# The last chunk of a graph layer with experts: slot tiles and sorting earlier, placing later, and a copy moved from VectorE to ScalarE

## The chip, the cores and the metric

The kernel runs on one core of a Trainium2 chip. The time is the device time of one execution in microseconds (us); the time of the kernel before is the median of three runs. The engines are called by their names in the profile: PE (TensorE), DVE (VectorE), ACT (ScalarE), POOL (GpSimd), and SP, whose queue issues plain DMAs. Each engine works through its own instructions in the order of the program.

## What is computed

The input has 6250 nodes of 256 features (x) and 100000 edges (src, dst), sorted by dst. All arithmetic is float32.

```python
h = layernorm(x)
agg = segment_sum(h[src], dst) / maximum(deg, 1)          # mean over a node's incoming edges
x = x + concat([h, agg], axis=1) @ W.T + b                # the graph layer
xn = layernorm(x) * gamma + beta                          # the feed-forward layer
top2 of (xn @ Wr + br) among 8 experts, softmax over the two
y_e = gelu(xn @ W1[e] + b1[e]) @ W2[e] + b2[e]            # 256 -> 512 -> 256
x = x + sum of the two chosen y_e, weighted
```

## The kernel before

**Windows, chunks, batches.** The edges are cut into 784 tiles of 128. Fourteen tiles make a window (a run of at most 128 consecutive destination nodes), 56 windows in all; four windows make a chunk, 14 chunks. For every edge tile POOL gathers 128 rows of the transformed nodes from DRAM (`gather`, L624) into one of 28 buffers `xg`, and PE adds them to the window's sums with a one-hot matrix (`add_edges`, L641). A gather reuses the buffer of the gather 28 places before it.

**From a finished chunk to its experts.** `window_done` plans the steps of a chunk. They are counted from its last edge tile: normalising, routing to two experts (`route`, `choices`), counting how many tokens each expert gets (`count_tokens`). Then, for each of the four windows, `one_hot_slots` (L719 to L722, DVE, two instructions into a tile `to`) builds the one-hot matrix that sorts the window's tokens by expert, and `sort_tokens` (L728 on PE, L731 on ACT) applies it and writes the sorted tokens to `xs`. On DVE `share_runs`, `place_rest` and `place_runs` work out where each expert's run of tokens goes. `copy_runs` (L872, ACT, eight groups of four copies, each group behind a load of registers) copies the runs to their places in `xe`. `find_rows` (L822, L826 to L835) works out for each token the rows of the results that it will need, `put_plan` (L839, SP, four times) writes that plan to DRAM, each at a row that depends on the data, and `load_plans` (L854) reads it back by node.

**Experts.** Each expert has a share of 128 slots in a chunk: `hidden` (L897 on PE, Gelu at L902 on ACT) and `result` (L910 on PE, bias at L914 on DVE, then a write to `y_d` through SP). Tokens beyond a share are collected over a batch of chunks into extra tiles. The batches are of 8, 5 and 1 chunks, with 8, 5 and 2 extra tiles. `more_stages` works on these tiles in three parts: `one` (L940: first product on PE; L944: a copy of it from PSUM to SBUF), `two` (L949: four transposes on PE; L952: Gelu on ACT) and `three` (L958: second product on PE; L962: bias on DVE; L965: write to `y_d` through SP). The PSUM tiles `ph` and `pm` have two buffers each, `py` has one. The five extra tiles of the second batch are called T0 to T4 here.

**Adding up.** When a batch is complete, its nodes can be finished in tiles of 128 nodes, n0 to n48: 27 tiles after the first batch, 18 after the second, 4 after the third. `gather_rows` reads the node's row (L986, SP) and issues two gathers of result rows on POOL (L989); `add_rows` makes two weighted additions on DVE (L996) and writes the output (L998, SP). The three buffers of a node tile come in turn from the same 28 `xg`, so the first gather of node tile n reuses the buffer from which the output of tile n-9 was written.

**The order of the work** is written by hand. For each edge tile, and after the last of them for further steps, `after` does this: first what was planned for the step with `at`, then expert tasks from a list as far as a budget of estimated us allows, then additions and gathers of finished nodes. The last chunk has its own step numbers in `LastSteps`: `hot` and `sort` for the four windows, `runs`, `rest` and `place` for the three placing functions, `copied` for the first `copy_runs` (one more group per step, `pace`), `rows` for `find_rows`, the plan writes one per step (`apart`) from `rows + 1`, `start` for the chunk's experts. What stands in the same step goes in the order in which it was planned: the slot tiles and sorts first, then placing, copying, rows, plan writes, and after all that the expert tasks. During the last chunk's steps the rest of chunk 12's experts and T0 to T4 are on the task list.

Of the kernel before, what the change touches and what calls it, by code (L numbers as in the profile page):

```python
# [8 lines left out]
F32 = mybir.dt.float32  # L9
I32 = mybir.dt.int32  # L10
AF = mybir.ActivationFunctionType
# [6 lines left out]
P = 128  # L18
# [4 lines left out]
CW = 4  # L23
# [10 lines left out]
def gnn_ffn_kernel(ctx: ExitStack, tc: tile.TileContext, x, x_cols, src, dst, dst_next, gw, gw_t, gb, gb_cols, gamma, beta,  # L34
# [35 lines left out]
    nc = tc.nc  # L70
# [542 lines left out]
    work = fast_pools.enter_context(tc.tile_pool(name="work", bufs=2, side="right"))  # L613
# [102 lines left out]
        nc.vector.tensor_scalar(q2, q2, -1.0, None, op0=ALU.add)  # L716

    def one_hot_slots(G, i):
        to = work.tile([P, 2 * P], F32, name="to", bufs=3)  # L719
        nc.vector.tensor_scalar(to, cols, G.to[:, 0, i:i + 1], None, op0=ALU.is_equal)  # L720
        nc.vector.scalar_tensor_tensor(to, cols, G.to[:, 1, i:i + 1], to, op0=ALU.is_equal, op1=ALU.add)  # L721
        G.one_hot[i] = to  # L722
# [155 lines left out]
    def in_turn(items, of):  # L878

        return [(us, f, of) for t in range(len(items) + 2) for d in range(3)  # L880
                if 0 <= t - d < len(items) and d < len(items[t - d]) for us, f in items[t - d][d]]
# [47 lines left out]
    def more_stages(B):  # L929

        def one(T):
            if T.first == 0:
                _, B.regs = nc.values_load_multi_w_load_instructions(
                    B.expert[0:1, :], engines=(ET.PE, ET.DVE, ET.Activation), min_val=0, max_val=NX - 1,
                    skip_runtime_bounds_check_because="clamped to it")
            T.e = B.regs[T.first]
            at = B.at + T.first * XS
            ph = ps.tile([P, H], F32, name="ph")
            for k in range(KD):
                nc.tensor.matmul(ph, xe[:, k, at:at + P],  # L940
                                 w1_sb[:, bass.ds(T.e, 1), k, :].rearrange("p a h -> p (a h)"),
                                 start=(k == 0), stop=(k == KD - 1))
            T.pre = slots.tile([P, H], F32, name="rows", bufs=3)
            nc.vector.tensor_copy(T.pre, ph)  # L944

        def two(T):
            pt = ps.tile([P, KH, P], F32, name="ph")
            for c in range(KH):
                nc.tensor.transpose(pt[:, c, :], T.pre[:, c * P:(c + 1) * P], ident)  # L949
            T.hid = slots.tile([P, KH, 2 * P], F32, name="hid")  # L950
            for c in range(KH):
                nc.scalar.activation(T.hid[:, c, :P], pt[:, c, :], AF.Gelu,  # L952
                                     bias=b1_sb[:, bass.ds(T.e, 1), c:c + 1].rearrange("p a c -> p (a c)"))

        def three(T):
            py = ps.tile([P, 2, D], F32, name="py", bufs=1)
            for c in range(KH):
                nc.tensor.matmul(py[:, 0, :], T.hid[:, c, :P],  # L958
                                 w2_sb[:, bass.ds(T.e, 1), c, :].rearrange("p a d -> p (a d)"),
                                 start=(c == 0), stop=(c == KH - 1))  # L960
            ys = slots.tile([P, 2, D], F32, name="rows", bufs=3)
            nc.vector.tensor_tensor(ys[:, 0, :], py[:, 0, :],  # L962
                                    b2_sb[:, bass.ds(T.e, 1), :].rearrange("p a d -> p (a d)"), op=ALU.add)
            at = B.more_row + T.first * XS
            nc.sync.dma_start(y_d[at:at + P, :], ys[:, 0, :])  # L965
            B.left -= 1

        items = []
        for i in range(B.tiles):
            T = Group()  # L970
            T.first = i
            items.append([[(1.7, lambda T=T: one(T))], [(0.5, lambda T=T: two(T))], [(1.75, lambda T=T: three(T))]])
        return in_turn(items, B)
# [32 lines left out]
    class Steps:  # L1006

        x1, var, roots, norms, route, exps, weigh, choices, count = 2, 5, 7, 9, 11, 14, 15, 16, 19
        hot, sort = (22, 24, 26, 28), (26, 28, 30, 32)
        runs, rest, place, tiles, copied, rows, pace, start, apart = 30, 33, 36, 39, 40, 46, 1.5, 60, 2  # L1010

    class LateSteps:

        x1, var, roots, norms, route, exps, weigh, choices, count = 2, 4, 5, 7, 9, 11, 12, 13, 15
        hot, sort = (17, 18, 20, 22), (19, 21, 23, 25)
        runs, rest, place, tiles, copied, rows, pace, start, apart = 20, 22, 24, 27, 26, 28, 1.25, 36, 1

    class LastSteps:

        x1, var, roots, norms, route, exps, weigh, choices, count = 2, 4, 5, 6, 7, 8, 9, 10, 12  # L1020
        hot, sort = (13, 14, 17, 18), (15, 16, 19, 20)
        runs, rest, place, tiles, copied, rows, pace, start, apart = 15, 16, 19, 24, 21, 22, 1, 29, 1

    def at(t, f, *args):
        later.setdefault(max(t, now), []).append(lambda: f(*args))
# [1 line left out]
    def window_done(V, G, K, t):  # L1027
# [26 lines left out]
        for m in range(CW):  # L1054
            at(t + S.hot[m], one_hot_slots, G, m)
            at(t + S.sort[m], sort_tokens, G, m)
# [134 lines left out]
    with tc.If(wrong_r > 0), tc.tile_pool(name="gp", bufs=1) as gp:  # L1191
# [9 lines left out]
        with tc.For_i(0, W * C) as j:  # L1201
# [22 lines left out]
            to = gp.tile([P, 1], I32, name="to")  # L1224
# [107 lines left out]
```

## Time and profile before

| | us |
|---|---|
| Three runs | 1191.4, 1193.38, 1197.1 |
| Median | 1193.38 |
| The profiled execution's own time | 1191.66 |
| Its span (first to last instruction) | 1189.9 |
| PE / DVE / ACT / POOL busy | 1056.3 / 691.0 / 465.4 / 844.3 |
| Mean granted clock of PE (1 is full) | 0.956 |

A line of the order in time holds the start in us from the span's start, the duration in us, the engine, the line of the kernel, the operation, what it writes and reads, the count, and in brackets the idle time of the engine before it with what ended it. An engine with a "q" is its queue's own work, such as issuing a DMA; the duration of such a line is that of issuing, not of the transfer. A line of the waits names who waited for whom, the sum in us, how often, and the longest. A line of the groups has busy time, mean ns of one instruction, and idle time before.

### The profile page before, as it was taken

The page shows a single profiled execution, that of the slowest core. Times are in us where ns is not written, and L with a number is a line of the kernel's source. Part 1 is how long each engine was busy: PE and PEld are TensorE (multiplying, and loading weights), DVE is VectorE, ACT ScalarE, POOL GpSimd, SP SyncE. Part 2 cuts the span into 40 slices and gives each one's busy share as a digit, 9 for nine tenths or more (in the row PEclk, how much of TensorE's full clock was granted, in tenths as well). Part 3 has the DMA queues.
Part 4 walks back from the last instruction along what each step waited for, and adds up shares of the span by engine and source line. Part 5 has one row for each costly group of instructions (what it writes and reads, how often), then busy time and mean ns, then how long its engine had stood idle before and what let it go on. Part 6 is the DMA issues. An engine that isn't in the chain of part 4 may idle for free.

```text
span 1189.9 us, 18885 instructions
## 1 busy us (share of the span) xinstructions
PE 1056.3 (89%) x5352; PEld 853.5 (72%) x5352; DVE 691.0 (58%) x2428; ACT 465.4 (39%) x1282; POOL 844.3 (71%) x892
## 2 busy tenths in 40 slices
PE   7959996599989899898998979899999999997970
PEld 6747873488868678685877858578888888785750
DVE  5858897365736555463565537465572745657642
ACT  3330013435444434443453444434553543643510
POOL 0077777777777777777777777777777777777575
PEclk9989997899999999998999999999999999998995
DMA  9988978856564554546456465555656565677784
GB/s 322 350 274 265 289 220 267 259 142 144 143 146 140 139 141 137 136 138 147 131 147 135 140 133 144 136 144 140 141 135 158 144 137 143 144 209 218 206 249 131
DMA packets 143578, 210.08 MB, mean 177 GB/s; under 512 B 36652, under 2 KB 111128, under 8 KB 143340
## 3 DMA queue, kind: packets, MB, share of 16 engines
q0 software_dynamic: 42768, 118.91, 40.6%
q1 hardware_dynamic: 92364, 80.45, 21.1%
q10 hardware_dynamic: 8336, 9.45, 2.4%
q8 instruction: 45, 0.74, 0.3%
q14 instruction: 65, 0.53, 0.2%
HBM read 163.86 MB, written 44.86 MB: 175 GB/s over the span
## 4 chain that ended last, share of the span: by engine, by line
PE 67%; DMA 15%; DVE 8%; issue 4%; ACT 3%; POOL 2%; ACTq 1%; POOLq 0%; SPq 0%; DVEq 0%
PE pS L641 23%; PE ph L897 15%; PE py L910 14%; DMA xg<-z_d,src_i 6%; DMA xg<-y_d,plans 4%; PE pm L728 4%; ACT xe L872 2%; PE ph L271 2%; PE pm L271 2%; PE pS L644 2%; PE py L958 2%; DMA plan_d<-plan 1%; PE ph L940 1%; DVE xg L996 1%; DMA xg<-x_dram,src_i 1%
## 5 line engine op out<-in xcount | busy, mean ns | idle before, releaser
L624 POOL DMA_INDIRECT xg<-z_d,src_i x770 | 732.8, 952 | 234.8 <-issue 111.0
L641 PE MATMUL pS<-xg,hot 128*128 128x265 f32 x1540 | 432.1, 404 | 42.0 <-DMA xg<-z_d,src_i 37.8
L641 PEld LDWEIGHTS pS<-xg,hot 128*128 128x128 f32 x1540 | 280.1, 194 | 127.3 <-DMA xg<-z_d,src_i 63.9
L897 PEld LDWEIGHTS ph<-xe,w_sb 128*128 128x128 f32 x1792 | 221.1, 196 | 23.9 <-ACT hid L902 10.2
L897 PE MATMUL ph<-xe,w_sb 128*128 128x128 f32 x1792 | 223.9, 280 | 13.7 <-ACT hid L902 9.8
L910 PE MATMUL py<-w_sb,hid 128*128 128x256 f32 x896 | 214.5, 383 | 1.7 <-DVE rows L914 1.7
L635 DVE TENSOR_TENSOR hot<-cols,rel 128x896 f32<-128x896 f32 x110 | 119.7, 1088 | 142.8 <-PE pS L641 140.2
L902 ACT ACTIVATE hid<-ph,b_sb 128x128 f32<-128x128 f32 x448 | 127.9, 369 | 172.3 <-PE ph L897 172.0
L910 PEld LDWEIGHTS py<-w_sb,hid 128*128 128x128 f32 x896 | 169.1, 191 | 33.3 <-issue 6.7
L872 ACT ACTIVATE xe<-xs x448 | 140.0, 313 | 98.3 <-ACT xe L872 32.6
L989 POOL DMA_INDIRECT xg<-y_d,plans x98 | 95.9, 978 | 37.9 <-issue 15.9
L731 ACT ACTIVATE xs<-pm,beta_sb,gamma_sb 128x256 f32<-128x256 f32 x112 | 57.3, 562 | 134.6 <-PE pm L728 132.1
L914 DVE TENSOR_TENSOR rows<-py,b_sb 128x512 f32<-128x512 f32 x56 | 38.4, 687 | 111.8 <-PE py L910 111.8
L728 PE MATMUL pm<-to,xn 128*128 128x256 f32 x224 | 58.8, 385 | 5.4 <-DVE to L721 5.4
L663 ACT ACTIVATE sums<-pS 128x265 f32<-128x265 f32 x55 | 21.4, 389 | 106.7 <-PE pS L641 99.2
L683 DVE SCALAR_TENSOR_TENSOR x<-pS,rdeg,x 128x264 f32<-128x264 f32 x55 | 27.1, 493 | 56.2 <-DMA x<-u_d 54.8
L996 DVE SCALAR_TENSOR_TENSOR xg<-xg,plans,xg 128x256 f32<-128x256 f32 (+1 forms) x98 | 45.8, 483 | 21.2 <-DMA xg<-y_d,plans 19.4
L271 PE MATMUL ph<-gc,x_t 128*128 128x264 f32 (+1 forms) x200 | 56.6, 407 | 1.4 <-ACT zt L295 0.9
L902 ACT ACT_TABLE_LOAD x25 | 32.1, 1283 | 64.7 <-PE ph L897 55.1
L339 POOL DMA_INDIRECT xg<-x_dram,src_i x14 | 13.5, 961 | 61.6 <-DMA src_i<-src_dram 57.6
L271 PE MATMUL pm<-gc,x_t 128*128 128x264 f32 (+1 forms) x192 | 53.1, 400 | 1.4 <-DVE u_t L425 1.4
L728 PEld LDWEIGHTS pm<-to,xn 128*128 128x128 f32 x224 | 42.7, 192 | 14.1 <-issue 4.7
(214 smaller groups left out, 908.0 us busy)
## 6 DMA issues: line engine op xcount, KB each, us to landing
y_d<-rows SPq DMA_DIRECT2D x56, 256.0 KB
xg<-z_d,src_i POOLq DMA_INDIRECT x770, 3.1
w_sb<-w_dram ACTq DMA_DIRECT2D x16, 512.0 KB
x<-u_d SPq DMA_DIRECT2D x55, 132.0 KB
x_d<-x SPq DMA_DIRECT2D x55, 128.0 KB
u_d<-u_t SPq DMA_DIRECT2D x24, 264.0 KB
x_t<-x_cols_dram SPq DMA_DIRECT2D x12, 512.0 KB
xu<-x_dram SPq DMA_DIRECT2D x24, 256.0 KB
```

The lines of the kernel that those rows point to most:

```text
L271: nc.tensor.matmul(pz, x_t[:, t, k, :], gc[:, h * KD + k, :n], start=(k == 0), stop=(k == KD - 1))
L624: nc.gpsimd.indirect_dma_start(out=xg[(g * C + c) % XG][:, :DZ], out_offset=None, in_=z_d[:, :], in_offset=bass.IndirectOffsetOnAxis(ap=sr ...
L635: nc.vector.tensor_tensor(hot, col[:, None, :].to_broadcast([P, HC, P]), V.rel[:, c:c + HC, None].to_broadcast([P, HC, P]), op=ALU.is_equal)
L641: nc.tensor.matmul(V.pS, V.hot[c // HC][:, c % HC, :], xg[(V.g * C + c) % XG], start=(c == 0), stop=(c == C - 1))
L728: nc.tensor.matmul(px[:, k, :], G.xn[i][:, k * P:(k + 1) * P], G.one_hot[i], start=True, stop=True)
L731: nc.scalar.activation(xs[:, at:at + 2 * P], px[:, k, :], AF.Identity, bias=beta_sb[:, k:k + 1], scale=gamma_sb[:, k:k + 1])
L872: nc.scalar.activation(xe[:, :, bass.ds(to_at, CAP)], src[:, :, bass.ds(src_at, CAP)], AF.Copy)
L897: nc.tensor.matmul(ph[:, i, a * SH:(a + 1) * SH], w1_sb[:, U.e + a, k, c * P:(c + 1) * P], xe[:, k, at:at + SH], start=(k == 0), stop=(k = ...
L902: nc.scalar.activation(U.hid[:, c, a * SH:(a + 1) * SH], ph[:, i, a * SH:(a + 1) * SH], AF.Gelu, bias=b1_sb[:, U.e + a, c:c + 1])
L910: nc.tensor.matmul(U.py[:, h, :], U.hid[:, c, h * P:(h + 1) * P], w2_sb[:, U.e + h, c, :], start=(c == 0), stop=(c == KH - 1))
L989: nc.gpsimd.indirect_dma_start(out=V.y2[r], out_offset=None, in_=y_d[:K.batch.end_row, :], in_offset=bass.IndirectOffsetOnAxis(ap=plans[:c ...
L996: nc.vector.scalar_tensor_tensor(V.o, V.y2[r], plans.bitcast(F32)[:count, n, 2 + r:3 + r], V.o, op0=ALU.mult, op1=ALU.add)
```

## The change

Three things are altered. The slot tile `to` has four buffers (`CW` is 4) where it had three. The copy of an extra tile's first product goes to ScalarE; it is the same line for all fifteen extra tiles. And the last chunk's step numbers are other ones: the four slot tiles stand in steps 13, 13, 14 and 15, the sorts in 14 to 17, the placing functions in 16, 17 and 18 where they were in 15, 16 and 19, and `copied`, `rows` and `start` are one step earlier. `tiles` stays in step 24.

```diff
     def one_hot_slots(G, i):
-        to = work.tile([P, 2 * P], F32, name="to", bufs=3)
+        to = work.tile([P, 2 * P], F32, name="to", bufs=CW)
...
             T.pre = slots.tile([P, H], F32, name="rows", bufs=3)
-            nc.vector.tensor_copy(T.pre, ph)
+            nc.scalar.activation(T.pre, ph, AF.Copy)
...
     class LastSteps:
 
         x1, var, roots, norms, route, exps, weigh, choices, count = 2, 4, 5, 6, 7, 8, 9, 10, 12
-        hot, sort = (13, 14, 17, 18), (15, 16, 19, 20)
-        runs, rest, place, tiles, copied, rows, pace, start, apart = 15, 16, 19, 24, 21, 22, 1, 29, 1
+        hot, sort = (13, 13, 14, 15), (14, 15, 16, 17)
+        runs, rest, place, tiles, copied, rows, pace, start, apart = 16, 17, 18, 24, 20, 21, 1, 28, 1
```

## The prediction

> **What bounds the kernel now.** I read the page's groups first, then who waited for whom on POOL, then the order in time of POOL and SP over the last 145 us.
>
> ```profile
> span 1189.9 us, 18885 instructions
> L624 POOL DMA_INDIRECT xg<-z_d,src_i x770 | 732.8, 952 | 234.8 <-issue 111.0
> L989 POOL DMA_INDIRECT xg<-y_d,plans x98 | 95.9, 978 | 37.9 <-issue 15.9
> ...
> POOL xg L624 <- issue: 111.0, 364, 0.3
> POOL xg L989 <- DVE xg L996: 6.3, 13, 2.0
> POOL xg L989 <- DMA out_dram<-xg: 5.3, 2, 5.0
> ```
>
> A gather costs POOL 0.95 us and 0.30 us to the next. No wait before the 770 edge gathers (L624) is over 0.3 us, so they follow one another every 1.253 us, whatever PE does, although PE has most of the chain of waits. Then come 98 gathers of result rows (L989), two for each of 49 node tiles. Only those have real waits.
>
> ```profile
> 1046.00 0.95 POOL L989 DMA_INDIRECT xg<-y_d,plans  x1 [0.30 <-issue]
> ...
> 1105.01 0.94 POOL L989 DMA_INDIRECT xg<-y_d,plans  x1 [1.27 <-DVE high L811]
> ...
> 1108.19 0.95 POOL L989 DMA_INDIRECT xg<-y_d,plans  x1 [0.99 <-DVE xg L996]
> ...
> 1115.44 0.95 POOL L989 DMA_INDIRECT xg<-y_d,plans  x1 [5.04 <-DMA out_dram<-xg]
> ...
> 1122.46 1.16 POOL L989 DMA_INDIRECT xg<-y_d,plans  x1 [1.99 <-DVE xg L996]
> ...
> 1177.75 1.77 POOL L989 DMA_INDIRECT xg<-y_d,plans  x1 [0.31 <-issue]
> ```
>
> Counted from 0, these are gathers 0, 46, 48, 50, 54 and 97. Beyond the usual 0.30, the four waits cost 0.97 + 0.69 + 4.74 + 1.69 = 8.1 us. Without them gather 54 would start at 1046.0 + 54 x 1.253 = 1113.7; with them it starts at 1122.46. From there 43 spacings take 55.3 us without a wait, and 12.1 us follow to the end. So the time is 1122.46 plus a fixed train: what moves gather 54 moves the end, one for one, and nothing else in this change can, unless it opens a new gap.
>
> Gather 54 is the first of node tile 27, so it needs the rows of the second batch's five extra tiles in y_d. Gathers 46, 48 and 50 reuse a buffer out of which an earlier output was written, so they need the writes at L998. Both go through SP:
>
> ```profile
> 1102.25 0.35 SPq L839 DMA_DIRECT2D plan_d<-plan  x1
> ...
> 1105.55 4.16 SPq L839 DMA_DIRECT2D plan_d<-plan  x2
> ...
> 1111.14 0.44 SPq L998 DMA_DIRECT2D out_dram<-xg  x1
> 1112.58 0.34 SPq L839 DMA_DIRECT2D plan_d<-plan  x1
> ...
> 1114.90 0.81 SPq L854 DMA_DIRECT2D plans<-plan_d  x2
> ...
> 1117.17 0.94 SPq L965 DMA_DIRECT2D y_d<-rows  x2
> ```
>
> The four plan writes overlap in memory as far as the program knows, so each stands in SP until the one before has landed: 3.3, 3.8 and 3.2 us from issue to issue, 2.3 to the read back. Output 16, behind the third, goes out at 1111.14 and gather 50 follows 4.3 us later. The last y_d rows go out at 1117.17 + 0.94 - 0.42 = 1117.69 and gather 54 follows 4.8 us later.
>
> **The change, part by part.** Orders come from stepping through the planner with the old and the new numbers: up to step +12 both are the same, and gathers, additions and extra tiles keep their places within a step.
>
> *Eight copies of the first batch* (L944 to ScalarE) lie among the edge gathers. There 28 buffers stand between POOL and PE, 28 x 1.253 = 35 us of lead, and the waits of 0.3 say that none of it is short. Cost 0; it would be visible only if PE fell behind by most of that lead.
>
> *The fourth buffer and the earlier one-hot tiles.* All four pairs (0.92 us each on DVE) now follow the count, which frees DVE at 1079.17 as before. In order on DVE until the copies may start: 4 pairs 3.7, three additions (n9 to n11) 2.9, one bias sum 0.7, share_runs 1.5, place_rest 3.0, place_runs 1.6, DVE's own register load 0.6, and 0.7 waiting for PE's last chunk-12 result: 14.7, so place_runs ends at 1093.9 against 1094.91. The four sorts run on PE and ACT by 1089, so the first copy_runs needs only place_runs and a register load (0.9 between load and first copy): 1094.8. Before, it stood behind sort 3's two evacuations and began at 1097.83. Gain there 3.0 us, off the path so far.
>
> *The copies of T0 to T4 on ScalarE.* The 128x512 ScalarE copy is not in the trace. Nearest rows: Copy of 265 columns 389 ns, Identity of 256 with pointers 562 ns. From 256 to 265 columns a Copy takes 385 to 389, so 512 lie between 0.49 (that slope) and 1.1 (twice the 562); the Copy row is the nearer, and I take 0.6 with DVE's 0.69 (L944) as a check.
> The Trainium skill ("ScalarE: Activation LUTs", What ACT_TABLE_LOAD costs) states 186 ns + 0.833 ns a column for such an ACTIVATE, an estimate of 0.61. Its Rules for kernel authors send simple elementwise work to VectorE rather than ScalarE, which speaks against the move: by that rule the five copies would only load the queue that sets T4.
> The ACT queue after: eight copy_runs groups of 1.34 = 10.7, register loads not covered by a Gelu or copy 3 x 0.42 + 2 x 0.2 = 1.7, Gelus of T1 and T2 2 x 1.05 = 2.1, copies of T3 and T4 1.2: 15.7, so 1094.8 becomes 1110.5 for the end of group 7 (before 1113.48). Then Gelu T3 to 1111.6, T4 to 1112.7 (before 1114.51). So PE's last products: T3 1110.9 to 1112.9 (1.97), DVE 0.42 and a py handover, T4 1113.5 to 1115.5, DVE to 1115.9, y_d at about 1116.0, gather 54 at 1116.0 + 4.8 = **1120.8**. Why not more: 3.0 us of earlier start less 1.2 of copies; T3 and T4 then wait for each other through the one py buffer.
>
> *DVE relieved of five copies* (3.4 us) reaches addition 14 at 1093.9 + two additions 1.9 + find_rows 1.9 + T0's sum 0.4 + 0.95 = 1099.1 (before 1100.41).
>
> *SP.* Output 14 at 1099.1, plan write 0 at 0.8 after it, 1099.9. But the fourth plan write, which followed output 16, now stands ahead of it and of T1's y_d: output 16 waits 3.3 + 3.8 + 3.2 = 10.3 us for three landings, then a write (0.45) and a load (0.45): 1111.1, against 1111.14. Gather 50 stays at 1115.4. The gain is behind it: output 17 follows at once, gathers 52 and 54 lose their ring waits, and four spacings of 1.253 put gather 54 at no earlier than **1120.4**. Output 18 and the y_d of T2 to T4 come after the plans are read, at 1112.4 to 1113.9, then 0.45 each: 1116 at the latest, as above.
> With three plan writes of 2.3 us, the shortest seen, gather 50 is at 1112.0; with three of 3.8, at 1116.5.
> The skill ("DMA: Bandwidth & Descriptors", Anatomy of one DMA) puts the fixed cost of a transfer at about 2 us, mostly the write's receipt. The rows above, 2.3 to 3.8, are longer under this load; with 2 us gather 50 would be at 1111.1, and T4's rows alone would set gather 54.
>
> *Sum.* Gather 54 at max(1120.4, 1120.8) = 1120.8, which is 1.7 us earlier; the train and the end behind it stay. The last chunk's experts also start 1 to 2 us earlier, but their last y_d write (1156.7) had to be ready for gather 90 at 1168.4: 1156.7 + 4.8 leaves 6.9 us unused, so this is worth nothing. The two extra tiles of the last batch are copied by an idle ACT: 0. The profiled run took 1191.66 (span 1189.9 and 1.8 around it), so 1190.0 for its like; the median of the three runs is 1.7 above it, 1193.4 - 1.7 = 1191.7.
>
> **The rivals.**
> *Nothing arrives* (1193.4): sorting ahead is idle work, since the copies wait for place_runs anyway, and T4's rows and the plan writes give back the rest. For it: three paths meet within 0.5 us at gather 54. It holds if the sum of three plan writes is 12 us instead of 10.3.
> *ACT becomes the queue that decides* (slower). Copies of T3 and T4 stand behind four and seven copy_runs groups, PE waits for them, and after idling 2.2 us before 1107.41 its eight L958 products took 3.39 instead of 1.97 us. With the first copy_runs as late as before (1097.83 + 15.7 = 1113.5), Gelu T3 from there, T3's product slowed (1113.9 to 1117.3), T4's to 1119.9, y_d 1120.4, gather 54 at 1125.2: +2.7, 1196.1. It decides once T4's y_d goes out after 1117.7. If both products are slow and each copy costs 1.1, 1.4 + 1.0 more: 1198.5.
> *All four POOL waits vanish* (faster): gather 54 at 1113.7 + 0.2, that is -8.6, 1184.8. It needs T4's rows out by 1109.1, while ACT's own work by the sum above ends at 1112.7; I see no row that allows it.
>
> **How the numbers follow.** Forecast (-4 to -0.5 us) 0.48, nothing (within 0.5 us of no change) 0.22, ACT decides 0.18, POOL waits mostly gone 0.12. 0.5%, about what a measurement of this kernel can tell from no change, is 6 us: the forecast, nothing, and half of the ACT case lie within it, with a little taken for scatter (the three runs differ by 5.7 us). Faster 0.14, same 0.74, slower 0.12. The range goes from 1186.0 (plan writes at their shortest, and part of the vanishing case) to 1198.0 (the dear end of the ACT case).
>
> **What would show it.** Right: gather 54 at 1119.5 to 1122; its longest wait of POOL still before gather 50, ended by an output write behind plan writes; copy_runs from about 1095; no wait among the last 44 gathers. Wrong: a first copy_runs after 1097, PE waiting over 2 us for a ScalarE copy, a gap in POOL after gather 54, or a gather 50 before 1113.

## The result, and the profile after

The changed kernel takes 1197.63 us (median of 22 runs, 1194.92 to 1202.0), the kernel before 1193.12 (22 runs, 1189.9 to 1198.16). The ratio is 1.0035, with an interval of 1.0024 to 1.0045: slower by some 4 us, where 1191.7 and a gain of 1.7 us were forecast. The profiled execution took 1199.39 us, its span is 1197.5 and PE's mean granted clock 0.949 (0.956 before).

The end is again tied to the result gathers on POOL. First the span and the two groups of gathers on the page, then the waits of the result gathers, in the form of those shown of before:

```profile
span 1197.5 us, 18908 instructions
L624 POOL DMA_INDIRECT xg<-z_d,src_i x770 | 733.7, 953 | 234.6 <-issue 107.5
L989 POOL DMA_INDIRECT xg<-y_d,plans x98 | 96.9, 989 | 45.1 <-issue 15.8
```

```profile
POOL xg L989 <- DMA out_dram<-xg: 10.8, 10, 4.0
POOL xg L989 <- DVE xg L996: 9.3, 12, 4.4
```

The edge gathers are as they were. The result gathers idle 7.2 us more than before (45.1 against 37.9), and the span is 7.6 longer. The order in time on POOL shows where; these are all gathers from 38 on whose wait is over the usual 0.30 or 0.31:

```profile
1101.57 0.94 POOL L989 DMA_INDIRECT xg<-y_d,plans  x1 [1.79 <-DVE mine L833]
1107.56 0.94 POOL L989 DMA_INDIRECT xg<-y_d,plans  x1 [1.27 <-DVE xg L996]
1113.67 0.95 POOL L989 DMA_INDIRECT xg<-y_d,plans  x1 [3.92 <-DMA out_dram<-xg]
1119.88 0.94 POOL L989 DMA_INDIRECT xg<-y_d,plans  x1 [4.01 <-DMA out_dram<-xg]
1129.03 0.97 POOL L989 DMA_INDIRECT xg<-y_d,plans  x1 [4.45 <-DVE xg L996]
```

They are gathers 42, 46, 48, 50 and 54. Gather 48 waits 3.92 us where it waited 0.99 (in control, a second execution of the kernel before further down, it waits 3.33), and gather 54 starts 6.6 us later than before. Behind it nothing waits, and 68.5 us are left to the end (67.4 before). What holds gathers 48, 50 and 54 is on SP, in order of time:

```profile
1103.00 0.38 SPq L998 DMA_DIRECT2D out_dram<-xg  x1
1103.88 4.06 SPq L839 DMA_DIRECT2D plan_d<-plan  x2
1108.71 0.38 SPq L998 DMA_DIRECT2D out_dram<-xg  x1
1110.35 3.53 SPq L839 DMA_DIRECT2D plan_d<-plan  x2
1113.97 0.39 SPq L965 DMA_DIRECT2D y_d<-rows  x1
1114.88 0.44 SPq L998 DMA_DIRECT2D out_dram<-xg  x1
...
1122.06 4.68 SPq L965 DMA_DIRECT2D y_d<-rows  x2
```

Output 15 (1108.71) now stands behind two plan writes, and T1's rows (1113.97) and output 16 behind all four. Who waits for T1's rows is what the prediction did not ask. The next lines, of DVE and PE, say why it matters:

```profile
1117.25 0.42 DVE L962 TENSOR_TENSOR rows<-py,b_sb 128x256 f32<-128x256 f32 x1 [9.22 <-DMA y_d<-rows]
...
1109.43 1.89 PE L958 MATMUL py<-w_sb,hid 128*128 x8
...
1117.82 3.75 PE L958 MATMUL py<-w_sb,hid 128*128 x8 [4.75 <-DVE rows L962]
1122.18 3.75 PE L958 MATMUL py<-w_sb,hid 128*128 x8 [0.61 <-DVE rows L962]
```

The kernel before had, of SP (T1's rows), DVE (T2's sum) and PE (the second products of T2, T3 and T4):

```profile
1109.80 0.77 SPq L965 DMA_DIRECT2D y_d<-rows  x1
...
1111.33 0.42 DVE L962 TENSOR_TENSOR rows<-py,b_sb 128x256 f32<-128x256 f32 x1 [3.06 <-PE py L958]
...
1107.90 3.39 PE L958 MATMUL py<-w_sb,hid 128*128 x8
...
1111.90 1.97 PE L958 MATMUL py<-w_sb,hid 128*128 x8
1114.47 1.97 PE L958 MATMUL py<-w_sb,hid 128*128 x8 [0.61 <-DVE rows L962]
```

In the changed kernel T2's second product is done at 1111.3, but its bias sum runs at 1117.25, where before it followed its product at once: it waits for a y_d write, that of T1's rows, because it takes the SBUF buffer out of which T1's rows are written. By the trace that write lands at 1117.16, 0.09 us ahead of the sum. The tag `rows` has three buffers, and L914, L944 and L962 draw from it. With L944 on ScalarE it is T2's sum that gets the buffer of T1's rows (here and in tail_act2 below), with L944 on VectorE it is T3's (in steps_only2 below); how the buffers are handed out was not looked into. PE then idles 4.75 us, since there is one `py`, and the products of T3 and T4 take 3.75 us each instead of 1.97: PE's granted clock is 0.50 from 1115.62 to 1125.84, where it was 1.00 from 1111.60 to 1117.00 in the kernel before.

Gather 50 alone would have let gather 54 start at 1119.88 + 4 x 1.253 = 1124.9, an estimate; T4's late rows cost 4.1 us beyond that.

### The profile page after: what moved, and what is told of

Its sections match the earlier page's. It is cut to its first block, busy times and chain, and to the rows that moved or that the text cites. A ratio compares the mean times of both kernels' runs of the same rounds, so it can differ in the third digit from the quotient of the medians.

```text
span 1197.5 us, 18908 instructions
## 1 busy us (share of the span) xinstructions
PE 1060.7 (89%) x5352; PEld 859.7 (72%) x5352; DVE 681.0 (57%) x2413; ACT 472.4 (39%) x1297; POOL 846.2 (71%) x892
## 4 chain that ended last, share of the span: by engine, by line
PE 68%; DMA 13%; DVE 9%; issue 3%; ACT 3%; POOL 2%; ACTq 0%; SPq 0%; POOLq 0%; DVEq 0%
PE pS L641 23%; PE ph L897 16%; PE py L910 15%; DMA xg<-z_d,src_i 6%; PE pm L728 4%; DMA plan_d<-plan 3%; PE ph L271 2%; PE py L958 2%; PE pS L644 2%; PE pm L271 2%; PE ph L940 2%; ACT xe L872 1%; DMA xg<-y_d,plans 1%; DMA xg<-x_dram,src_i 1%; DVE st L195 1%
## 5 line engine op out<-in xcount | busy, mean ns | idle before, releaser
L641 PE MATMUL pS<-xg,hot 128*128 128x265 f32 x1540 | 432.1, 404 | 40.5 <-DMA xg<-z_d,src_i 38.2
L641 PEld LDWEIGHTS pS<-xg,hot 128*128 128x128 f32 x1540 | 283.9, 196 | 123.4 <-DMA xg<-z_d,src_i 56.2
L897 PEld LDWEIGHTS ph<-xe,w_sb 128*128 128x128 f32 x1792 | 222.7, 197 | 23.3 <-ACT hid L902 12.2
L897 PE MATMUL ph<-xe,w_sb 128*128 128x128 f32 x1792 | 225.7, 282 | 13.2 <-ACT hid L902 11.8
L910 PEld LDWEIGHTS py<-w_sb,hid 128*128 128x128 f32 x896 | 170.6, 193 | 33.5 <-issue 6.8
L872 ACT ACTIVATE xe<-xs x448 | 139.4, 311 | 95.3 <-ACT xe L872 35.8
L989 POOL DMA_INDIRECT xg<-y_d,plans x98 | 96.9, 989 | 45.1 <-issue 15.8
L914 DVE TENSOR_TENSOR rows<-py,b_sb 128x512 f32<-128x512 f32 x56 | 38.5, 687 | 113.0 <-PE py L910 113.0
L683 DVE SCALAR_TENSOR_TENSOR x<-pS,rdeg,x 128x264 f32<-128x264 f32 x55 | 27.1, 493 | 75.4 <-DMA x<-u_d 73.9
L996 DVE SCALAR_TENSOR_TENSOR xg<-xg,plans,xg 128x256 f32<-128x256 f32 (+1 forms) x98 | 45.5, 482 | 19.8 <-DMA xg<-y_d,plans 17.3
```

The lines of the kernel that those rows point to most:

```text
L641: nc.tensor.matmul(V.pS, V.hot[c // HC][:, c % HC, :], xg[(V.g * C + c) % XG], start=(c == 0), stop=(c == C - 1))
L872: nc.scalar.activation(xe[:, :, bass.ds(to_at, CAP)], src[:, :, bass.ds(src_at, CAP)], AF.Copy)
L897: nc.tensor.matmul(ph[:, i, a * SH:(a + 1) * SH], w1_sb[:, U.e + a, k, c * P:(c + 1) * P], xe[:, k, at:at + SH], start=(k == 0), stop=(k = ...
L910: nc.tensor.matmul(U.py[:, h, :], U.hid[:, c, h * P:(h + 1) * P], w2_sb[:, U.e + h, c, :], start=(c == 0), stop=(c == KH - 1))
L989: nc.gpsimd.indirect_dma_start(out=V.y2[r], out_offset=None, in_=y_d[:K.batch.end_row, :], in_offset=bass.IndirectOffsetOnAxis(ap=plans[:c ...
L996: nc.vector.scalar_tensor_tensor(V.o, V.y2[r], plans.bitcast(F32)[:count, n, 2 + r:3 + r], V.o, op0=ALU.mult, op1=ALU.add)
```

## The experiments

Three theories. **A:** T2's sum waits for a buffer that T1's rows are still being written from. **B:** the eight first-batch copies on ScalarE make PE's products in the edge stage late for good, so the last chunk is counted later. **C:** the new steps put the plan writes ahead of output 15, output 16 and T1's rows in SP's queue. Each kernel was timed beside runs of the kernel before on its chip.

### Two chips that tell no times apart

Eight of the runs fell on two chips on which everything takes 20% longer: the kernel before 1430.43 us on one (runs from 1415.7 to 1440.8) and 1426.63 on the other.

own_rows is the changed kernel with the extra tiles' results in buffers of their own, and three slot tiles again:

```diff
-        to = work.tile([P, 2 * P], F32, name="to", bufs=CW)
+        to = work.tile([P, 2 * P], F32, name="to", bufs=3)
...
-            ys = slots.tile([P, 2, D], F32, name="rows", bufs=3)
+            ys = (work, work, slots)[T.first % 3].tile([P, 1, D], F32, name=("raw", "raw_t", "third")[T.first % 3], bufs=1)
```

> The changed kernel, but the five results T0 to T4 (and the other extra tiles' results) are written into three 1 KB buffers of their own instead of the three buffers 'rows' that they share with the copies; 'to' has three buffers again to make room. Theory A (the shared buffers): the bias sum of T2 (L962) no longer waits 9.2 us for T1's write to y_d, it starts when its product is done, about 1112 instead of 1117.3; gather 54 moves from 1129.0 to 1122 to 1125 and the time from 1197.6 to 1193 to 1195. Theory B (the eight copies of the first batch made PE 3 us late for the rest of the run) and theory C (the fourth plan write ahead of output 16 and T1's rows): the time stays within 1 us of 1197.6.

mid_act is the kernel before with ScalarE copies for the first batch only:

```diff
-            nc.vector.tensor_copy(T.pre, ph)
+            nc.scalar.activation(T.pre, ph, AF.Copy) if B.first == 0 else nc.vector.tensor_copy(T.pre, ph)
```

> The kernel before with only the first batch's eight copies (L944) moved to ScalarE. Theory B: PE's lead over the gathers falls by about 3 us around 765 us and stays so, the last chunk's count comes 2 to 3 us later, and the time rises by 1.5 to 3.5 us, to 1194.6 to 1196.6. Theories A and C: no change, within 1 us of 1193.1.

tail_act is the kernel before with ScalarE copies for all but the first batch:

```diff
-            nc.vector.tensor_copy(T.pre, ph)
+            nc.vector.tensor_copy(T.pre, ph) if B.first == 0 else nc.scalar.activation(T.pre, ph, AF.Copy)
```

> The kernel before with only the copies of T0 to T4 and of the last batch's two tiles moved to ScalarE, old steps. Theory A: the sum of T2 waits for T1's y_d write, which goes out at 1109.8 as before, so until about 1113.8 instead of 1111.3; PE idles meanwhile and two products take 3.4 to 3.8 us; gather 54 at 1125 to 1127, time 1195.5 to 1198. Theories B and C: within 1 us of 1193.1.

steps_only is the changed kernel with all copies on VectorE:

```diff
-            nc.scalar.activation(T.pre, ph, AF.Copy)
+            nc.vector.tensor_copy(T.pre, ph)
```

> The kernel before with the new steps and four buffers for 'to', copies left on VectorE. Theory C: outputs 15 and 16 stand behind two and four plan writes, gather 50 at 1118 to 1120 instead of 1115.4, time 1195 to 1197. Theories A and B: no loss; by the prediction's own sum the first copy_runs moves from 1097.8 to about 1095 and the time falls by 0 to 2 us, to 1191 to 1193.

Measured: own_rows 1.0053 (1.0015 to 1.0090), mid_act 1.0039 (1.0003 to 1.0076), tail_act 1.0057 (1.0023 to 1.0091), steps_only 1.0037 (0.9997 to 1.0078).

On the second chip: the changed kernel again; mid_dve, the changed kernel with the first batch's copies on VectorE (L944 as in tail_act); far_plan, whose edit puts the last chunk's plan writes 12 steps later and the load of its plans with them (the node numbers are still set where they were); and far_own_mid, which is far_plan, mid_dve and own_rows in one.

```diff
-            at(t + S.rows + 1 + m * S.apart, put_plan, G, m)
+            at(t + S.rows + 1 + m * S.apart + (12 if S is LastSteps else 0), put_plan, G, m)
```

after_again: 

> The changed kernel itself, on the chip of the three runs beside it. All theories: about 0.35% (4.2 us) over the kernel before, interval about 0.2 to 0.5%; T2's bias sum (L962) again waits for the write of T1's rows, and two plan writes stand ahead of output 15.

mid_dve: 

> The changed kernel with the eight first-batch copies back on VectorE; the copies of T0 to T4 and of the last batch stay on ScalarE, and the steps stay new. Theory B (the eight copies make TensorE's products about 3.1 us late for good, so that the last chunk's counts come 2 to 3 us later): the lead of TensorE over the edge gathers is again that of before, the count starts about 2.5 us earlier than in the changed kernel, and the time is 2.5 to 3 us under the changed kernel, some 0.12% over the kernel before. Theory A (only T2's wait for T1's write decides): the lead comes back, but the wait of the L962 sum for the write is there still and gather 54 comes at most 0.5 us earlier: 0.3% over the kernel before. Theory C (the plan writes ahead of output 15 and of T1's rows): the writes come with the count, so it goes with B in the count's 2.5 us and keeps the 4-us waits of gathers 48 and 50.

far_plan: 

> The changed kernel with the last chunk's four plan writes and the load of its plans issued 12 steps later, behind the rows of all five tiles on SP's queue. Theory C: output 15 goes out at once (some 4 us earlier) and T1's rows as well, T2's sum waits some 4 us less, TensorE's gap ahead of T3's second products falls from 4.75 us to about 1, and gather 54 comes 3 to 4 us earlier: about level with the kernel before (-0.05 to +0.1%). Theory A with C: the wait on the rows buffer is the step, and the plan writes are what feeds it: the same time. Theory B: the steps are late from TensorE on, the write's place only moves waits about among gathers 48, 50 and 54: at most 1 us under the changed kernel, 0.25 to 0.35% over the kernel before. If the plans' load comes too late for gather 90, POOL waits there and the time is over the changed kernel's.

far_own_mid: 

> The new steps and the ScalarE copies of T0 to T4 and of the last batch, but without each of the three suspects: the eight first-batch copies on VectorE, the extra tiles' results in buffers of their own (with three one-hot buffers), and the plan writes behind the rows of the five tiles. A, B and C together: T2's sum waits for no write, the count is back at the time of before, and gather 54 comes about 2 us ahead of its place before: 1 to 3 us under the kernel before (-0.1 to -0.25%). If the copies on ScalarE or the sort steps cost by themselves, by another way than A, B and C: still 0.15% or more over the kernel before.

Measured: after_again 1.0040 (1.0010 to 1.0070), mid_dve 1.0054 (1.0022 to 1.0086), far_plan 1.0104 (1.0055 to 1.0154, six runs), far_own_mid 1.0052 (1.0021 to 1.0082). The changed kernel loses the same 0.4% here, but all eight come out 0.37 to 1.04% over the kernel before, whatever they undo, and all their intervals overlap, with runs of one kernel up to 29.5 us apart (steps_only). They tell no theory from another. Nor is the reasoning on POOL valid there: the edge gathers are no fixed train, since POOL waits for PE. These are lines of the waits of after_again:

```profile
POOL xg L624 <- PE pS L641: 145.6, 127, 7.5
POOL xg L624 <- remote: 61.1, 39, 5.5
```

Its longest wait before an edge gather is 7.5 us; in the first comparison none is over 0.3. What these traces do show is the mechanism of A: T2's sum waits for the write in after_again and tail_act (8.63 and 4.39 us idle ahead of it) and not in own_rows, where it follows PE. Why far_plan, which gains below, lost 1% here stays open: its six runs reach from 1427.29 to 1449.68, and the one that was profiled is the fastest, level with the kernel before.

### Each part alone, on a chip like the first

control is the kernel before, unchanged. mid_act2 and tail_act2 are mid_act and tail_act once more. far_own_dve has the new steps, all copies on VectorE, and the edits of own_rows and far_plan.

control: 

> The kernel before, word for word, run as if it were another one. All theories: level with the kernel before, within 0.3%. It shows how far two samples of one kernel lie apart, and gives a trace of the kernel before on the chip of the three runs beside it. Should it come out 0.3 to 0.5% over, then no difference of that size in the runs beside it stands for anything.

mid_act2: 

> The kernel before with the eight first-batch copies on ScalarE, once more. Theory B: TensorE's products in the edge stage end about 3 us later from the first batch's extra tiles on, so the time is 2.5 to 3 us (0.2%) over the kernel before where the edge stage sets the end, and the tail behind the last edge product is as long as before. Rivals A and C: level.

tail_act2: 

> The kernel before with the copies of T0 to T4 and of the last batch's two tiles on ScalarE, once more, beside a trace of the kernel before on the same chip. Theory A: T2's bias sum waits for the write of T1's rows (4 us and more), the control's doesn't, and gather 54 comes 2 to 4 us later relative to the last edge product: 0.2 to 0.4% over the kernel before. Theories B and C: level within 0.2%.

far_own_dve: 

> The new steps alone, with every copy of a first product on VectorE, the extra tiles' results in buffers of their own (three one-hot buffers) and the plan writes behind the rows of the five tiles. If the copies on ScalarE cost by themselves (in what far_own_mid kept of them: T0 to T4 and the last batch's two): level with the kernel before or up to 3 us under it. If the new steps cost by themselves, since they put four one-hot pairs and sorts among the last edge tiles: 0.3 to 0.6% over the kernel before, as far_own_mid.

Measured beside 1193.71 of the kernel before: control 1194.26, 1.0001 (0.9984 to 1.0019); mid_act2 1195.4, 1.0008 (0.9993 to 1.0024); tail_act2 1194.67, 1.0015 (0.9999 to 1.0031); far_own_dve 1189.44, 0.9966 (0.9949 to 0.9982).

So neither group of copies is shown to cost anything by itself: 1.0008 and 1.0015, and both intervals take in no change, though that of tail_act2 (to 1.0031) also reaches into that of the loss (from 1.0024). B's mechanism is there nevertheless. These lines are two of PE's first products (L940) for the first batch's extra tiles, in the order in time of mid_act2:

```profile
762.05 3.68 PE L940 MATMUL ph<-w_sb,xe 128*128 x4 [2.06 <-ACT xe L872]
769.66 1.98 PE L940 MATMUL ph<-w_sb,xe 128*128 x4 [2.15 <-ACT xe L872]
```

The same two in the kernel before:

```profile
763.63 1.98 PE L940 MATMUL ph<-w_sb,xe 128*128 x4 [1.39 <-ACT xe L872]
768.94 1.98 PE L940 MATMUL ph<-w_sb,xe 128*128 x4 [1.54 <-ACT xe L872]
```

PE waits for a copy_runs (L872) that now stands behind the ScalarE copy, 0.6 to 0.7 us longer per tile, and one product runs at half speed (3.68 us; the granted clock is 0.50 from 762.13 to 765.50). PE's lead over the gathers (from the last product that reads a buffer to the gather that reuses it, median of 28) falls around these tiles from 28.7 to 22.9 us before and from 29.8 to 24.2 in the control, but from 28.5 to 19.7 in the changed kernel and from 30.1 to 21.0 in mid_act2: 3.2 us more, and it does not come back. The two longer waits and the slower product are 3.0 us of that; a fall of 7.3 (29.6 to 22.3) in tail_act2, whose first-batch copies are on VectorE, shows that it varies between executions. By its time, mid_act2 puts this at 1 us, with an interval of -0.8 to +2.9.

A's wait is there in tail_act2 too, but the sum comes 3.2 us after its product (at 1112.07) and not 5.9, since with the old steps three plan writes stand ahead of T1's rows and not four:

```profile
1115.29 0.42 DVE L962 TENSOR_TENSOR rows<-py,b_sb 128x256 f32<-128x256 f32 x1 [4.84 <-DMA y_d<-rows]
```

### Taking each cause out of the changed kernel

steps_only2, own_rows2 and far_plan2 are steps_only, own_rows and far_plan once more; far_before is the kernel before with far_plan's edit and nothing else. The changed kernel itself was not run again on these chips; its ratio is that of the first comparison, 1.0035 (1.0024 to 1.0045).

steps_only2: 

> The new steps alone, every copy of a first product on VectorE, shared rows buffers, once more, on a chip like that of the first comparison if it comes to one. Theory C (the order on SP): all four plan writes stand ahead of T1's rows and two ahead of output 15, gathers 48 and 50 wait as in the changed kernel, gather 54 is 1 to 3 us later than in the control (1124.3): +0.1 to +0.25%. Theory A (T2's wait for T1's write alone): T2's sum doesn't wait here, so gather 54 is at the control's place: within 0.1%. Theory B: level, since the eight copies are on VectorE; with B and A alone true, the steps are worth 0.

own_rows2: 

> The changed kernel with the extra tiles' results in buffers of their own and three one-hot buffers, once more. Theory A: T2's sum waits for no write, the half-speed products of T3 are gone, and gather 54 moves from 1129.0 up to the bound that gather 50 gives (1119.9 and four gathers: 1124.9), so 3 to 4 us under the changed kernel, +0 to +0.1% over the kernel before. Theory B: at most 1.5 us of it, +0.2 to +0.3%, as the late counts stay. Theory C: T1's rows and output 16 stay behind four plan writes, gathers 48 and 50 still wait 3.5 to 4 us, and so the gain ends at the bound of gather 50.

far_plan2: 

> The changed kernel with the last chunk's plan writes and their load behind the rows of the five tiles on SP, once more. Theory C: T1's rows go out some 4 us earlier, gathers 48 and 50 wait for no output, T2's sum waits 4 us less, gather 54 comes at 1121 to 1124 and the time is 5 to 7 us under the changed kernel: -0.05 to -0.25% against the kernel before. Theory B: gather 54 stays 2 to 3 us behind that of a kernel with the eight copies on VectorE. Theory A without C (the write itself is slow, not its place in the queue): T2's wait stays at 4 us or more and gather 54 at 1126 or later: +0.1% or more.

far_before: 

> The kernel before with nothing but the last chunk's plan writes and their load moved behind the rows of the five tiles on SP: no new steps, no copy on ScalarE. Theory C: SP's order costs the kernel before as well (output 16 and T1's rows behind three plan writes), gathers 48 and 50 lose their waits of 3 to 4 us and gather 54 comes 2 to 4 us ahead of the control's: -0.2 to -0.35%, as far_own_dve, so that far_own_dve's gain is the queue's and not the steps'. If the new steps bring the gain of far_own_dve: -0.1% or less.

Measured beside 1194.13 of the kernel before: steps_only2 1194.21, 0.9998 (0.9983 to 1.0013); own_rows2 1194.26, 0.9993 (0.9980 to 1.0006); far_plan2 1191.05, 0.9973 (0.9957 to 0.9989); far_before 1191.01, 0.9979 (0.9962 to 0.9996).

The buffers alone take the whole loss out of the changed kernel, with the steps, the plan writes and all fifteen ScalarE copies left as they are (a fourth slot tile had no room beside them; the fourth tile is not what costs, since far_plan2 and steps_only2 have it). Of own_rows2, DVE, PE and POOL:

```profile
1111.11 0.42 DVE L962 TENSOR_TENSOR third<-py,b_sb 128x256 f32<-128x256 f32 x1 [3.52 <-PE py L958]
...
1113.88 1.99 PE L958 MATMUL py<-w_sb,hid 128*128 x8 [0.88 <-ACT hid L952]
1116.49 1.97 PE L958 MATMUL py<-w_sb,hid 128*128 x8 [0.61 <-DVE raw L962]
...
1113.81 0.95 POOL L989 DMA_INDIRECT xg<-y_d,plans  x1 [5.01 <-DMA out_dram<-xg]
1118.94 1.18 POOL L989 DMA_INDIRECT xg<-y_d,plans  x1 [2.94 <-DVE raw_t L962]
```

T2's sum follows its product at once, the products take 1.97 us again, and after gather 50 (1118.94) no gather waits: gather 54 comes at 1124.62, where gather 50 lets it.

Moving the plan writes alone takes the loss out as well and more. Of far_plan2, SP, DVE and POOL:

```profile
1103.08 0.32 SPq L965 DMA_DIRECT2D y_d<-rows  x1
1108.95 0.32 SPq L965 DMA_DIRECT2D y_d<-rows  x1
1113.76 2.89 SPq L965 DMA_DIRECT2D y_d<-rows  x2
...
1108.50 0.42 DVE L962 TENSOR_TENSOR rows<-py,b_sb 128x256 f32<-128x256 f32 x1 [3.61 <-PE py L958]
...
1118.85 1.05 POOL L989 DMA_INDIRECT xg<-y_d,plans  x1 [4.39 <-DVE xg L996]
```

T1's rows go out 0.03 us after their sum ends, and land at 1106.51, so the shared buffer is free when T2's sum wants it. Gathers 48 and 50 have no wait left, and gather 54 waits for T4's rows alone: it starts 2.5 us after they go out (1116.33).

With the new steps alone (steps_only2) T2's sum takes another buffer, which is free; it is T3's that meets T1's late rows, 3.3 us, and gather 54 is not moved beyond where gather 50 puts it. T3's sum in steps_only2, 0.09 us behind the landing of T1's rows (1116.99):

```profile
1117.08 0.42 DVE L962 TENSOR_TENSOR rows<-py,b_sb 128x256 f32<-128x256 f32 x1 [3.31 <-DMA y_d<-rows]
```

So the steps alone cost nothing that shows, the copies alone most likely less than the loss, and either cure alone takes the loss out: the late write and the other buffer make it together.

### What is left when both are cured

far_own_act is the changed kernel with the edits of own_rows and far_plan; far_own_before is the kernel before with far_plan's edit and the buffers of own_rows.

far_own_act: 

> The changed kernel with both faults of its end cleared at once: the last chunk's plan writes and their load behind the rows of the five tiles, and the tiles' results in buffers of their own (three one-hot buffers); all copies on ScalarE, new steps. Theory A with C: either cure alone frees T2's sum, so the second adds nothing to far_plan2: -0.2 to -0.3%, gather 54 at 1118 to 1121. Theory B: 1 to 3 us over far_own_dve (-0.34%) for the eight copies. If A and C were two separate costs, it would be 2 us or more under far_plan2: -0.45% or lower.

far_own_before: 

> The kernel before with the plan writes and their load moved as in far_before, and the tiles' results in buffers of their own as well: old steps, all copies on VectorE. In far_before no sum waits for a write, so the buffers are worth nothing by theory A: -0.15 to -0.3%, gather 54 at 1117 to 1119. If the new steps are worth something by themselves, this stays 1 us or more over far_own_dve (-0.34%); if nothing, it is level with it within 0.15%.

Measured beside 1193.45: far_own_act 1189.75, 0.9980 (0.9964 to 0.9995); far_own_before 1190.28, 0.9977 (0.9956 to 0.9997). With far_before, far_plan2 and far_own_dve these are five kernels with the plan writes moved, at 0.9966 to 0.9980, with overlapping intervals. So A and C are one chain, not two sums, and the gain of some 0.25% is that of the queue's order: old steps or new, copies on VectorE or ScalarE, make no difference that shows. On chips like the first all five beat both kernels; far_before does so with the smallest edit.

The places of the steps in the profiled executions, in us from the start of the last edge gather (it shifts by up to 4 us between executions), worked out from the starts in the traces:

| kernel | first slot tile | T1's rows out | T2's sum | gather 50 | T4's rows out | gather 54 | gather 54 to the end | ratio of the times |
|---|---|---|---|---|---|---|---|---|
| before | 34.4 | 65.1 | 66.6 | 70.7 | 72.9 | 77.7 | 67.4 | 1 |
| control | 33.5 | 66.8 | 67.4 | 73.0 | 75.2 | 79.8 | 68.7 | 1.0001 |
| after | 38.2 | 70.4 | 73.7 | 76.4 | 82.9 | 85.5 | 68.5 | 1.0035 |
| mid_act2 | 37.2 | 68.1 | 70.9 | 73.8 | 77.0 | 81.8 | 68.3 | 1.0008 |
| tail_act2 | 35.6 | 65.7 | 70.0 | 72.6 | 77.1 | 80.7 | 68.5 | 1.0015 |
| steps_only2 | 36.0 | 68.2 | 66.5 | 73.9 | 75.3 | 79.1 | 68.7 | 0.9998 |
| own_rows2 | 35.1 | 67.4 | 64.8 | 72.7 | 74.0 | 78.3 | 68.2 | 0.9993 |
| far_plan2 | 36.0 | 60.3 | 65.7 | 67.0 | 73.6 | 76.1 | 67.8 | 0.9973 |
| far_own_act | 36.5 | 58.9 | 64.4 | 65.1 | 72.1 | 74.7 | 68.3 | 0.9980 |
| far_own_dve | 34.7 | 61.3 | 65.7 | 66.8 | 73.0 | 75.5 | 68.7 | 0.9966 |
| far_before | 32.9 | 59.6 | 64.8 | 65.4 | 70.5 | 73.4 | 68.4 | 0.9979 |
| far_own_before | 34.3 | 62.2 | 67.7 | 67.1 | 73.4 | 76.0 | 68.7 | 0.9977 |

From gather 54 to the end it is the same within 1.3 us in all twelve, so the time goes with gather 54. Its column puts the changed kernel last and the five with the plan writes moved first, as the ratios do; inside these groups single executions scatter (before and control are one kernel and differ by 2.1).

## Why the prediction was wrong, step by step

**Right: the frame.** What moves gather 54 moves the end, and no new gap opened behind it: gather 54 came 6.6 us later and the 68.5 us behind it stayed within 1.1 of those before. The control gives a second sample of before, with gather 54 at 1124.29; from there to 1129.03 are 4.7 us, about the 4.5 between the two medians.

**Right: the price of the copy.** The ScalarE copy takes 594 ns on average where 0.6 was taken, against 686 on DVE. The Trainium skill ("ScalarE: Activation LUTs", What ACT_TABLE_LOAD costs) would make it 0.61 us, in agreement. Its Rules for kernel authors send simple elementwise work (relu, max, min, add, mul; a copy is not listed) to VectorE; this copy out of PSUM is shorter on ScalarE, and the measurement decides.

**Wrong, and decisive: the way from T3's Gelu to T4's rows.** The sum took T3's product from ACT alone ("T3 1110.9 to 1112.9", rows at "about 1116.0") and gave T2's sum no wait. It followed engines and the PSUM tile, but not the SBUF tag `rows`, although the tag stands in both lines, L944 and L962. Measured: T2's sum 5.9 us after its product, T3's and T4's products 3.75 instead of 1.97, T4's rows out at 1126.42 instead of 1116.0. own_rows2, which removes this wait (and has three slot tiles again), has T4's rows at 1120.24 and no loss. POOL's longest wait was forecast before gather 50; it came before gather 54, 4.45 us.

**Wrong, and its feeder: what the fourth plan write is moved past.** The text saw that it "now stands ahead of it and of T1's y_d" and priced that only for output 16; who waits for T1's y_d was not asked. Output 15, which is now behind two plan writes too, was not named at all: gather 48, at 1108.19 before, came at 1113.67. The price itself was good: four writes and the way to output 16 took 1103.88 to 1114.88, 11.0 us, where 1099.9 to 1111.1 was forecast. Only it began 4 us late. The section of the skill that the prediction names for 2 us is on DMAs that GpSimd issues; these writes go through SP, and the four landed 3.7, 2.7, 3.2 and 1.4 us after they went out.

**Wrong: "place_runs ends at 1093.9", first copy_runs at 1094.8.** It began at 1098.79, past the 1097 that the prediction had named as a sign of being wrong. Of the 4.0 us, 2.6 are that the first slot tile stood at 1081.75 and not at 1079.17, and 1.4 are the sum behind it (17.0 instead of 15.6 from slot tile to copy). The first is in part the next point: from the last edge gather, the first slot tile comes 35.1 to 38.2 us later in the five kernels of the table with the first batch's copies on ScalarE and 32.9 to 36.0 in the seven without, 36.6 against 34.5 on average.

**Wrong: "Cost 0" for the first batch's eight copies.** The lead of 35 us hides PE's delay from POOL, as the text said, but not from the last chunk, whose sums are PE's last edge products: a lead that is spent is still a delay at the end of the stage. Mis-sized by 3.2 us of lead; by mid_act2's time it is worth 1 us (-0.8 to +2.9).

**Wrong as a price: 4.8 us from T4's rows to gather 54.** The trace keeps when a write lands and when POOL passes each of its waits. In the kernel before, T4's rows land at 1121.60, 3.9 us after they go out, POOL passes the wait for them at 1121.63, and gather 54 starts 0.86 us after the landing. So the 1.99 us that the view puts down to "DVE xg L996" ended with this write, and were no ring wait, as the prediction has it: output 18, whose buffer gather 54 takes, had landed at 1119.54. In the changed kernel T4's rows land 1.7 us after they go out, and gather 54 starts 0.94 us after that. The 4.8 us were thus the landing of that execution and no fixed duration: over the kernels of the table T4's rows take 3.8 to 3.9 us to land in before, control and mid_act2, 2.8 to 2.9 in tail_act2 and own_rows2, and 1.7 to 2.1 in the other seven, among them all five with the plan writes moved. So part of what that move gains is the faster landing. What makes it faster was not tried by itself.

The rival nearest to what came, ACT as the deciding queue, gave 1196.1 with "T3's product slowed (1113.9 to 1117.3)". The slow products were foreseen there, but with another cause: it was not ACT, which finished its last Gelu at 1115.71, but the buffer, and T4's product was slow as well.

## What to carry to other kernels

When an instruction moves to another engine or place, list every buffer tag it draws from, and who else draws from it: which buffer each of them gets can change, and a buffer's release may hang on a DMA that has just been pushed back in a queue. When a DMA is moved ahead of others, ask for each one that it passes who waits for it to land, not only for the first. And before tuning the work around a queue, try moving what nobody needs soon out of the way: on chips like the first that was the one edit that gained.

## What the runs showed of the hardware

Two of the chips ran the same kernel 20% slower (1426.63 and 1430.43 against 1193 to 1194). In after_again the mean granted clock of PE is 0.896 and its page books 75 us of idle time ahead of L897 to "issue", where that of the changed kernel on the other chip has 13.2 us of idle ahead of it in all. What causes it was not found.

PE's products run at half speed where the granted clock is 0.50: eight L958 products took 3.75 us in the changed kernel (0.50 from 1115.62 to 1125.84), 3.44 in tail_act2 (0.50 from 1115.44 to 1118.84) and 3.15 in steps_only2 (0.50 from 1118.30 to 1121.65, from within the products on), against 1.97 to 1.99 at 1.00. PE had idled 4.75, 2.02 and 2.68 us just ahead of them, while 1.99 was measured behind 1.81 in far_own_dve. The Trainium skill ("TensorE: Matmul & The Clock Gate", What's actually happening) puts the return to half clock after an idle window of about 3.4 us. The 4.75 agree with that; the 2.02 and 2.68 lie under it, and there the measurement decides.
